# A two-layer approximate-product convolution on one core: images closed two images later, first loads and weight preparation reordered

## The chip, the cores and the metric

The kernel runs on one core of one Trainium2 chip. The core has five engines that work side by side, each through its own list of instructions in order: TensorE (PE in the profile, with PEld for its weight loads), VectorE (DVE), ScalarE (ACT), GpSimd (POOL) and SyncE (SP), which here only issues transfers. They wait for one another by semaphores. The metric is device time in microseconds (us) of one launch; lower is better.

## The reference

The input x has 16 images of 256 channels, 28 x 28, in float32. Each image is group-normalized (32 groups), goes through two convolution layers and comes back with residuals. A layer replaces the 3x3 convolution by centroids: for each channel the nine values of a patch are compared with 16 centroids, a softmax over the negative squared distances gives 16 weights, and the output is the weighted sum of table rows.

```python
d = sum(p*p) - 2*einsum('bncs,cks->bnck', p, centroids) + sum(centroids**2)
attn = softmax(-d, axis=-1)
lut = einsum('cks,cso->cko', centroids, w_sub)
out = einsum('bnck,cko->bno', attn, lut)
```

Layer 1: this, then batch normalization and relu. Layer 2: this on layer 1's result, batch normalization, a squeeze-and-excitation gate (mean over the image, two small matrices, relu, sigmoid), then relu(gated + normalized x) and once more + x. That last line of elementwise work is called the closing of an image below.

## The kernel before

**Tiling.** An image and layer make four blocks: two halves of the channels (hh) times two halves of the rows (t). A block goes through two steps ("clusters" in the code, two per block, eight per image), so image number n of a layer-ordered count (0 to 15 in layer 1, 16 to 31 in layer 2) has its first step at g = 8 n.

**One block.** Patches are loaded from a padded copy in DRAM (`home1`, `home2`) into two buffers `pts` (L317). PE computes logits in eight banks of PSUM (L331), ACT takes exponentials (L348), PE makes the denominator and ninth numerator (`num_b`, L391) and the others (`num_a`, L378). ACT splits the denominator (`split_b`, L405), DVE joins it, takes the reciprocal (L423) and spreads it (L431); ACT copies or DVE scales the numerators (L448, L453), POOL scales the rest (`scale_q`, L444). A block leaves nine operands q of 128 x 392.

**One image.** The four blocks' operands and the 2 x 2 blocks of the weight matrix are multiplied by a Strassen-like scheme of seven products (table `PRODUCTS`, L42). POOL makes the operand differences (`mix`, L470, instructions at L472 and L474), DVE adds and subtracts the results (L499), and ACT normalizes them (L511). Products of image n run in steps g+5 to g+12, so they overlap with the next image's blocks. A product's bank in PSUM is free again when DVE or ACT has read it.

**Order.** Nothing is scheduled by a planner: every piece is entered with `at(step, place, function, ...)` (L813), and the pieces are emitted sorted by step and place (L1001). Each engine executes its instructions in that order, and tile buffers add the waits. A place below 0.5 is logits and the like, 0.5 patch loads, 1.3 to 1.8 the denominators and the spreading, 2.0 the product, 2.5 the mixes. Execution lags the nominal step on some engines.

**Where the change touches.** Loads of the next x (`load_x`, L133) go into the one buffer `xt`. The closing in layer 2 is `finish_norm`, `finish_gate`, `finish_relu` on ACT (L758, L754, L771), `finish_sum` and `finish_add` on POOL (L766, L774) and `store` on SP (L785); the last image instead has `finish_fast` on DVE (L777). Its four output tiles `y` share a ring of four with the padded tiles of layer 1; its normalized x (`xn`) uses tag `pb`, of which there is one buffer, as do the staging tiles `st` and `c2`, layer 2's transposition `z` and the flags' `ok`. In layer 2 the blocks with hh = 0 have a row maximum subtracted for a quarter of their logits (`wide_copy`, `wide_turn`, `wide_sub`, `wide_back`, `wide_exp`).

Layer 2's weights are permuted and prepared during layer 1: `prep_wd*`, `prep_cw*` (L644 to L693) on DVE with loads and stores by SP, and `sums_load`, `sums_put` (L695, L709) with sums on POOL. Layer 1's matrices are combined on DVE at the start (`combine`, L179; `center`, L245; `setup_bn`, L231, which goes back and forth between POOL and DVE).

Of the kernel before, what the change touches and what calls it, by code (L numbers as in the profile page):

```python
# [8 lines left out]
F32 = mybir.dt.float32  # L9
# [8 lines left out]
P = 128  # L18
H = W = 28
HW = H * W  # L20
# [3 lines left out]
N = RT * W  # L24
# [43 lines left out]
def kernel(  # L68
# [20 lines left out]
    nc = tc.nc  # L89
    B, C, _ = x.shape  # L90
    NB = C // P
# [11 lines left out]
    def bank(name):  # L103
        return p_ring.tile([P, 512], F32, tag="ps", name=name)
# [10 lines left out]
    d_cwb = dram.tile([P, 1024], F32, name="d_cwb")  # L115
# [10 lines left out]
    io = ctx.enter_context(tc.tile_pool(name="io", bufs=1))  # L126
    wpool = ctx.enter_context(tc.tile_pool(name="wpool", bufs=1))
    epool = ctx.enter_context(tc.tile_pool(name="epool", bufs=6))
# [1 line left out]

    xs = {}

    def load_x(b, eng=None):  # L133
        t = io.tile([P, NB, HW], F32, tag="xt", name="xt")
        (eng or nc.sync).dma_start(t, x[b].rearrange("(b p) n -> p b n", p=P))
        xs[b] = t

    def load_x0(k):
# [66 lines left out]
    pts = [const.tile([P, 8, PTW], F32, name=f"pt{i}") for i in range(NPT)]  # L205
# [9 lines left out]
    nc.gpsimd.memset(mhalf, -0.5)  # L215
    nc.vector.memset(xpads[0], 0.0)
    nc.gpsimd.memset(xpads[1], 0.0)
    nc.vector.memset(pts[0], 1.0)
    nc.gpsimd.memset(pts[1], 1.0)

    def rsqrt(dst, src, eps, n):
# [42 lines left out]
    def gn_stats(b, k):  # L264
        if k == 0:
            gst[b] = (
                small.tile([P, NB, 2, 6], F32, name="gn_st"),
                small.tile([P, NB, 2], F32, name="gn_mv"),
            )
        st, mv = gst[b]  # L270
        for i in range(2):
            nc.vector.bn_stats(st[:, k, i, :], xs[b][:, k, i * (HW // 2) : (i + 1) * (HW // 2)])
        nc.vector.bn_aggr(mv[:, k, :], st[:, k])

    def gn_mean(b, k0=0, n=NB):
        st, mv = gst[b]
        ps = bank("gnp")[:, : 2 * n]
        nc.tensor.matmul(
            ps, lhsT=gmat, rhs=mv[:, k0 : k0 + n].rearrange("p b t -> p (b t)"), start=True, stop=True
        )  # L280
        gm = small.tile([P, NB, 2], F32, name="gn_gm")
        nc.vector.tensor_copy(gm[:, :n].rearrange("p b t -> p (b t)"), ps)
        dv = small.tile([P, NB], F32, name="gn_dv")
        nc.vector.tensor_sub(dv[:, :n], mv[:, k0 : k0 + n, 0], gm[:, :n, 0])
        nc.vector.tensor_mul(dv[:, :n], dv[:, :n], dv[:, :n])
        gst[b, "m"] = gm, dv
# [16 lines left out]
    def gn_apply(b, k):  # L303
        nc.scalar.activation(
            grid(xpads[k])[:, 1 : H + 1, 1 : W + 1], xs[b][:, k].rearrange("p (r w) -> p r w", w=W), AF.Identity,
            bias=nrm[:, b, 2, k : k + 1], scale=nrm[:, b, 1, k : k + 1],
        )
# [305 lines left out]
    pw = {}  # L613
# [68 lines left out]
            nc.vector.tensor_scalar(f[:, :, 8 * c : 8 * c + 8], src[:, :, 0:8], m_cw[:, c : c + 1], None, op0=ALU.mult)  # L682
        nc.sync.dma_start(d_cwa, st[:, 512:1536])

    def prep_cwb():
        st = pw.pop("st")
        src = st[:, : 32 * S].rearrange("p (m i s) -> p m i s", i=4, s=S)
        f = st[:, 512:1536].rearrange("p (m i n) -> p m i n", i=4, n=32)
        for m in range(8):
            nc.vector.tensor_copy(f[:, m], m_b[:, m % 4, :].unsqueeze(1).to_broadcast([P, 4, 32]))  # L690
            nc.vector.tensor_mul(f[:, m], f[:, m], src[:, m, :, 8:9].to_broadcast([P, 4, 32]))
            nc.vector.tensor_add(f[:, m], f[:, m], ones_b[:, m % 4, :].unsqueeze(1).to_broadcast([P, 4, 32]))
        nc.sync.dma_start(d_cwb, st[:, 512:1536])  # L693

    def sums_load(k0):  # L695
        st = stage()
# [116 lines left out]
    def at(cl, sub, f, *a, **kw):  # L813
        jobs.setdefault((cl, sub), []).append((f, a, kw))
# [7 lines left out]
    for j, u in enumerate(blocks):  # L822
        gi, g = 8 * (j // 4), 2 * j
# [11 lines left out]
    for j, u in enumerate(blocks):  # L835
        g = 2 * j
        u["w"] = j
        wide = u["l"] == 1 and u["hh"] == 0
        for p in range(2):
            u["pt", p] = pts[p]  # L840
            at(g + p - NPT, 0.5, patches, u, p, nc.gpsimd if g + p < 5 else None)
            for q in range(2):
                mm = 2 * p + q
# [25 lines left out]
    for l in range(2):  # L869
        for b in range(B):  # L870
            n = l * B + b
            g = 8 * n
            us = blocks[4 * n : 4 * n + 4]
            for c, (w, r, ks) in PRODUCTS.items():
                at(g + c, 2.0, product, (n, c), us[r], w, ks)
            for mm in (4, 2, 3, 0, 1):
                at(g + 5, 2.5, mix, us[0], mm, us[1], us[0])
                at(g + 7, 2.5, mix, us[1], mm, us[2], us[1])
                at(*((g + 7, 2.6) if l == 0 else (g + 8, 1.0)), mix, us[0], mm, us[2], us[0])
                at(g + 10, 2.5, mix, us[0], mm, us[0], us[3])  # L880
            c11, c12, c21, c22 = (0, 0), (0, 1), (1, 0), (1, 1)
            at(g + 6, 0.0, acc_copy, l, b, c11, (n, 5))
            at(g + 7, 0.0, acc_copy, l, b, None, (n, 6))
            at(g + 8, 0.0, acc_add, l, b, None, (n, 7))
            at(g + 9, 0.0, acc_add, l, b, c21, (n, 8), c11)
            at(g + 10, 0.0, acc_add, l, b, c22, (n, 9), c11, pop=False)
            at(g + 10, 0.01, acc_add, l, b, c21, (n, 9))
            at(g + 10, 0.05, reg_add, l, b, c12, c22, None)
            at(g + 10, 0.06, reg_add, l, b, c22, c21, None)
            at(g + 11, 0.0, acc_add, l, b, c12, (n, 10))  # L890
            at(g + 11, 1.9, norm_out, l, b, *c12)
            at(g + 11, 1.91, norm_out, l, b, *c22)
            at(g + 12, 0.0, acc_add, l, b, c11, (n, 11))
            at(g + 12, 0.3, norm_out, l, b, *c11)
            at(g + 13, 0.0, acc_add, l, b, c21, (n, 12), op=ALU.subtract)
            at(g + 13, 0.3, norm_out, l, b, *c21)
            if l == 0:
                for o in range(2):
                    if b == 0:
                        at(g + 12 + o, 0.35, rank_score, o)  # L900
                        at(g + 12 + o, 0.6, rank_keep, o)
                        at(g + 12 + 2 * o, 0.65, h0_keep, o)
                    else:
                        for r in range(2):
                            at(g + 12 + o + (o and r), (0.5, 2.9)[r] if o == 0 else (2.4, 2.9)[r], to_home2, b, o, r)
                if b + 1 < B:
                    at(*((g - 1, 2.6) if b else (1, 0.7)), load_x, b + 1)
                    for q in range(NB):
                        at(g + (1 if b else 2) + 2 * q, 1.95, gn_stats, b + 1, q)
                    at(g + 4, 1.05 if b else 1.96, gn_mean, b + 1)  # L910
                    at(g + 4, 1.33 if b else 1.97, gn_var, b + 1)
                    for q in range(NB):
                        at(g + 5, 0.9, gn_apply, b + 1, q)
                        at(g + 5, 1.9, to_home1, b + 1, q)
            else:
                at(g + 10, 2.6, load_x, b)
                at(g + 13, 2.1, se_hidden, b)
                at(g + 14, 1.05, se_gate, b)
                for q in range(NB):
                    at(g + 13, 0.9, finish_norm, b, q)  # L920
                    if b < B - 1:
                        at(g + 15, 0.3, finish_gate, b, q)
                        at(g + 15, 0.9, finish_sum, b, q)
                        at(g + 16, 1.9, finish_relu, b, q)
                        at(g + 17, 0.05, finish_add, b, q)
                        at(g + 17, 2.9, store, b, q)
                    else:
                        at(g + 14, 1.92, finish_fast, b, q)
                        at(g + 14, 1.92, store, b, q)
                if b == B - 1:  # L930
                    at(g + 11, 0.95, flags)
                    at(g + 12, 2.9, flag_sum)

    at(2, 0.6, load_w, 0, "A11")
    at(3, 0.6, load_w, 0, "S3")
    at(3, 0.6, load_w, 0, "A22")
    at(5, 0.6, load_w, 0, "A12")
    for n, m in enumerate(("S1", "S2", "S4", "S3")):
        at((4, 5, 7, 6)[n], 1.95, combine, m)
    for hh in range(2):  # L940
        at(6, 2.7, keep_wd, hh)
    for o in range(2):
# [6 lines left out]
    for o in range(2):  # L949
# [5 lines left out]
        for part in range(3):  # L955
            c = 28 + 6 * o + 2 * part
# [4 lines left out]
    at(43, 1.05, prep_wd2)  # L961
    at(46, 0.6, prep_cw0)
    at(47, 1.9, prep_cwa)
    at(48, 1.9, prep_cwb)
    for n in range(5):
        at(50 + 2 * n, 0.6, sums_load, 2 * n)
        at(51 + 2 * n, 2.3, sums_put, 2 * n)
    g = 8 * B
    at(g - 2, 0.4, load_wd, 1, 0)
    at(g, 0.4, load_wd, 1, 1)  # L970
# [9 lines left out]

    for k in range(NB):
        gn_stats(0, k)
        gn_mean(0, k, 1)
        gn_var(0, k, 1)
        gn_apply(0, k)
        if k == 0:
            to_home1(0, 0)
# [4 lines left out]
    center_wd(0)  # L992
    at(-0.5, 0.7, to_home1, 0, 1)
    at(0, 0.6, load_wd, None, 1)
    at(1, 0.6, load_cw, 0, 1)
    at(1, 1.95, center_wd, 1)
    at(3, 1.95, setup_bn)
    for t in hpads:
        at(0, 1.95, nc.gpsimd.memset, t, 0.0)

    for key in sorted(jobs):  # L1001
        for f, a, kw in jobs[key]:
# [5 lines left out]
    with tc.If(rv > 0):  # L1008
        with tc.For_i(0, B, 1) as it:
            t = io.tile([P, NB, HW], F32, tag="xt", name="xt")  # L1010
# [13 lines left out]
            for l in range(2):  # L1024
# [6 lines left out]
                for t2 in range(2):  # L1031
                    us = []
# [125 lines left out]
```

## Time and profile before

| | us |
|---|---|
| time, median of three runs (lowest to highest) | 2848.76 (2846.7 to 2851.04) |
| the profiled execution: its own time | 2846.91 |
| the profiled execution: span from first to last instruction | 2845.4 |
| PE busy in matmuls | 2713.7 |
| POOL busy | 2055.2 |
| DVE busy | 1755.4 |
| ACT busy | 1456.7 |

The profile is one execution, recorded by the hardware. Busy time is that of instructions proper; waiting and the issuing of transfers are not counted. A group line of the profile reads: line of the code, engine, operation, output<-inputs, shape, count | busy us, mean ns of one | idle time of that engine just before, and what ended it. A line of the order of time reads: start, duration, engine, line, operation, tiles, shape, count. A line of the table by stage gives a window of the span, its length, the busy us and instruction count of PE, PE's weight loads, DVE, ACT and POOL, the granted PE clock as a share of full speed, the share of time that the DMA engines were busy, and GB/s. Matmul ends are modelled, so a busy PE is not necessarily at its peak.

### The profile page before, as it was taken

To read this page: it belongs to the slowest core of one execution; us is meant where nothing else is said; L and a number is where in the kernel's file an instruction comes from. 1 tells how busy PE (TensorE), PEld (TensorE's weight loads), DVE (VectorE), ACT (ScalarE), POOL (GpSimd) and SP (SyncE) were. 2 spreads that over 40 slices of the span, in tenths; PEclk is the share of its full clock that TensorE was granted. 3 is DMA by queue.
4 is the path that set the end of the run, shared out by engine and by line. 5 is a ranking of instruction groups with operands and counts; after the bars stand their busy time and mean duration, and the time that the engine had idled before them with its cause. 6 is when DMAs were issued, how large, how long until landed. Compare 5 with 4: busy or idle time off the path is not lost.

```text
span 2845.4 us, 87952 instructions
## 1 busy us (share of the span) xinstructions
PE 2713.7 (95%) x37076; PEld 1284.5 (45%) x37076; DVE 1755.4 (62%) x3973; ACT 1456.7 (51%) x3278; POOL 2055.2 (72%) x1396
## 2 busy tenths in 40 slices
PE   4789999999999999999999999999999999999997
PEld 1344444444444444444444444444444444444443
DVE  4656555675555556555657676666666667766664
ACT  3344455444555544445545556655555555555552
POOL 3647877668776676767667877777977778877776
PEclk8899999999999999999999999999999999999999
DMA  8565677567666655566665544544544555544541
GB/s 193 127 125 120 175 194 189 142 145 182 160 161 159 153 141 126 145 159 149 154 152 112 113 110 100 119 108 109 116 102 104 118 109 114 116 97 109 117 108 36
DMA packets 223009, 374.51 MB, mean 132 GB/s; under 512 B 30136, under 2 KB 193320, under 8 KB 222608
## 3 DMA queue, kind: packets, MB, share of 16 engines
q1 hardware_dynamic: 215376, 334.50, 51.8%
q0 software_dynamic: 7232, 34.30, 3.5%
q8 instruction: 296, 4.85, 0.8%
q14 instruction: 105, 0.86, 0.1%
HBM read 288.91 MB, written 79.80 MB: 130 GB/s over the span
## 4 chain that ended last, share of the span: by engine, by line
PE 61%; POOL 20%; DVE 11%; ACT 4%; issue 2%; DMA 2%; SPq 0%; DVEq 0%; POOLq 0%; ACTq 0%
PE acc L465 32%; PE lg L336 12%; POOL qp L474 11%; PE nb L397 8%; PE na L383 8%; POOL qp L446 3%; ACT e L348 3%; DVE r L423 3%; POOL y L767 2%; DVE rb L438 2%; POOL qo L472 1%; POOL z L368 1%; DVE se_gt L750 1%; DMA pt<-home 1%; DVE qp L457 1%
## 5 line engine op out<-in xcount | busy, mean ns | idle before, releaser
L348 ACT ACTIVATE e<-lg 128x392 f32<-128x392 f32 x1920 | 778.2, 526 | 934.3 <-PE lg L336 934.2
L474 POOL TENSOR_TENSOR qp<-qp,qp 128x784 f32<-128x784 f32 x512 | 936.8, 1864 | 0.0
L465 PE MATMUL acc<-qp,w_S 128*128 128x392 f32 x2048 | 737.6, 502 | 35.4 <-POOL qp L474 35.4
L446 POOL TENSOR_TENSOR qp<-qp,rb 128x784 f32<-128x784 f32 x256 | 472.6, 1869 | 299.3 <-DVE rb L438 299.2
L336 PE MATMUL lg<-pt,wd 32*32 32x392 f32 x16384 | 539.6, 505 | 31.3 <-DVE hpad L502 11.3
L465 PEld LDWEIGHTS acc<-qp,w_S 128*128 128x128 f32 x2048 | 375.8, 190 | 380.7 <-POOL qp L474 123.7
L438 DVE STREAM_SHUFFLE rb<-r 128x392 f32<-128x392 f32 x1024 | 540.5, 605 | 0.0
L465 PE MATMUL acc<-qp,w_A 128*128 128x392 f32 x1536 | 522.3, 493 | 0.2 <-POOL qp L474 0.2
L383 PE MATMUL na<-e,cwa 64*32 64x392 f32 x8192 | 408.6, 498 | 13.2 <-issue 7.4
L465 PEld LDWEIGHTS acc<-qp,w_A 128*128 128x128 f32 x1536 | 292.1, 190 | 215.2 <-POOL qp L474 1.4
L397 PE MATMUL nb<-e,cwb 64*32 64x392 f32 x8192 | 374.1, 500 | 0.0
L336 PEld LDWEIGHTS lg<-pt,wd 32*32 32x32 f32 x16384 | 231.6, 103 | 289.0 <-issue 187.9
L446 POOL TENSOR_TENSOR qo<-qo,rb 128x392 f32<-128x392 f32 x128 | 131.2, 1025 | 316.5 <-DVE rb L434 316.3
L457 DVE TENSOR_TENSOR qp<-na,rb 128x392 f32<-128x392 f32 x512 | 253.1, 558 | 150.5 <-PE na L383 150.3
L423 DVE RECIPROCAL r<-r 128x392 f32<-128x392 f32 x128 | 331.8, 2593 | 0.0
L417 DVE SCALAR_TENSOR_TENSOR r<-nb,kst,r 128x392 f32<-128x392 f32 x128 | 79.8, 623 | 375.9 <-ACT r L408 367.7
L383 PEld LDWEIGHTS na<-e,cwa 64*32 64x32 f32 x8192 | 143.2, 106 | 235.8 <-ACT e L348 119.7
L397 PEld LDWEIGHTS nb<-e,cwb 64*32 64x32 f32 x8192 | 146.6, 108 | 203.1 <-issue 130.9
L451 ACT COPY qp<-na 128x392 f32<-128x392 f32 x512 | 210.8, 505 | 7.1 <-PE na L383 7.1
L408 ACT ACTIVATE r<-nb,kst 128x392 f32<-128x392 f32 x128 | 86.9, 679 | 108.7 <-PE nb L397 103.7
L502 DVE TENSOR_TENSOR y<-acc,y 128x392 f32<-128x392 f32 x80 | 43.5, 561 | 148.7 <-PE acc L465 142.3
L472 POOL TENSOR_TENSOR qo<-qo,qo 128x392 f32<-128x392 f32 x128 | 131.7, 1029 | 0.5
(142 smaller groups left out, 1807.3 us busy)
## 6 DMA issues: line engine op xcount, KB each, us to landing
pt<-home SPq DMA_DIRECT2D x768, 209.0 KB
pt<-home SPq DMA_DIRECT2D x753, 104.5 KB
home<-xpad SPq DMA_DIRECT2D x32, 899.0 KB
xt<-in_x SPq DMA_DIRECT2D x31, 784.0 KB
out_dram<-y SPq DMA_DIRECT2D x32, 392.0 KB
w_S<-d_wS SPq DMA_DIRECT2D x4, 576.0 KB
st<-in_wsub SPq DMA_DIRECT2D x4, 512.0 KB
st<-d_wa SPq DMA_DIRECT2D x16, 128.0 KB
```

The costliest lines, as they stand in the source:

```text
L336: nc.tensor.matmul(bk[32 * c : 32 * c + 32, :N].rearrange("p (r w) -> p r w", w=W), lhsT=wts["wd", u["hh"]][32 * i : 32 * i + 32, mm, c, : ...
L348: nc.scalar.activation(eg[:, i, :], bk[:, :N], AF.Exp, scale=2.0)
L383: nc.tensor.matmul(bs[r][32 * i : 32 * i + 32, :N], lhsT=wts["cwa", u["hh"]][64 * r : 64 * r + 64, mm, i, :], rhs=es[64 * r : 64 * r + 64, ...
L397: nc.tensor.matmul(bs[r][32 * i : 32 * i + 32, :N], lhsT=wts["cwb", u["hh"]][64 * r : 64 * r + 64, mm, i, :], rhs=es[64 * r : 64 * r + 64, ...
L423: nc.vector.reciprocal(u["r"], u["r"])
L438: nc.vector.stream_shuffle(rb[:, r, :], u["r"], mask_of(2 * mm + r))
L446: nc.gpsimd.tensor_tensor(q, q, u.pop(("rb", mm)), ALU.mult)
L451: nc.scalar.copy(u["q", 2 * mm + r], bk[:, :N])
L457: nc.vector.tensor_mul(u["q", 2 * mm + r], bk[:, :N], rb[:, r, :])
L465: nc.tensor.matmul(accs[key][:, :N], lhsT=wl[w][:, k, :], rhs=us["q", k], start=first and n == 0, stop=last and n == len(ks) - 1,)
L472: nc.gpsimd.tensor_tensor(out_u["q", 8], in0["q", 8], in1["q", 8], ALU.subtract)
L474: nc.gpsimd.tensor_tensor(pair(out_u, mm), pair(in0, mm), pair(in1, mm), ALU.subtract)
```

## The change

Five things are done, all by other places in the order and two helper functions:

- Layer 2's closing: x is loaded at g+13 instead of g+10; norm and gate run at step g+19, sum and relu at g+20, add and store at g+21, where they were at g+13 to g+17. The last image keeps its own short closing, and its x goes into a spare tile of the exponentials' pool at g+11.
- The third mix of an image is put behind the next image's first pieces for the last image of layer 1 too, as for layer 2 (the condition was on the layer, and is now n < B - 1).
- At the start: one memset moves behind the first statistics; the second centring, the loads of A11, A12, cwa/cwb and image 1, image 1's group statistics, the four combinations and setup_bn get other steps.
- `prep_cwb`'s 24 operations are split into four parts of six in steps 48 to 51, and the loads and sums after it move two steps on.
- The zeroing of the padded tiles moves from step 0 to step 1.

```diff
-    def load_x(b, eng=None):
-        t = io.tile([P, NB, HW], F32, tag="xt", name="xt")
-        (eng or nc.sync).dma_start(t, x[b].rearrange("(b p) n -> p b n", p=P))
+    def load_x(b, spare=False):
+        if spare:
+            t = epool.tile([P, 4, N], F32, tag="e", name="e").rearrange("p i n -> p (i n)")
+            t = t.rearrange("p (b n) -> p b n", b=NB)
+        else:
+            t = io.tile([P, NB, HW], F32, tag="xt", name="xt")
+        nc.sync.dma_start(t, x[b].rearrange("(b p) n -> p b n", p=P))
...
-    nc.vector.memset(pts[0], 1.0)
...
-    def prep_cwb():
-        st = pw.pop("st")
+    def prep_cwb(part):
+        st = pw["st"]
...
-        for m in range(8):
+        for m in range(2 * part, 2 * part + 2):
...
-        nc.sync.dma_start(d_cwb, st[:, 512:1536])
+        if part == 3:
+            pw.pop("st")
+            nc.sync.dma_start(d_cwb, st[:, 512:1536])
...
-                at(*((g + 7, 2.6) if l == 0 else (g + 8, 1.0)), mix, us[0], mm, us[2], us[0])
+                at(*((g + 7, 2.6) if n < B - 1 else (g + 8, 1.0)), mix, us[0], mm, us[2], us[0])
...
-                    at(*((g - 1, 2.6) if b else (1, 0.7)), load_x, b + 1)
+                    at(g + (-1 if b else 2), 2.6, load_x, b + 1)
                     for q in range(NB):
-                        at(g + (1 if b else 2) + 2 * q, 1.95, gn_stats, b + 1, q)
-                    at(g + 4, 1.05 if b else 1.96, gn_mean, b + 1)
-                    at(g + 4, 1.33 if b else 1.97, gn_var, b + 1)
+                        at(g + (1 + 2 * q if b else 4), 1.95, gn_stats, b + 1, q)
+                    at(g + (4 if b else 5), 1.05, gn_mean, b + 1)
+                    at(g + (4 if b else 5), 1.33, gn_var, b + 1)
                     for q in range(NB):
-                        at(g + 5, 0.9, gn_apply, b + 1, q)
+                        at(g + 5, 0.9 if b else 1.5, gn_apply, b + 1, q)
                         at(g + 5, 1.9, to_home1, b + 1, q)
             else:
-                at(g + 10, 2.6, load_x, b)
+                last = b == B - 1
+                at(*((g + 11, 0.6) if last else (g + 13, 2.6)), load_x, b, last)
...
-                    at(g + 13, 0.9, finish_norm, b, q)
-                    if b < B - 1:
-                        at(g + 15, 0.3, finish_gate, b, q)
-                        at(g + 15, 0.9, finish_sum, b, q)
-                        at(g + 16, 1.9, finish_relu, b, q)
-                        at(g + 17, 0.05, finish_add, b, q)
-                        at(g + 17, 2.9, store, b, q)
+                    at(g + (13 if last else 19), 0.9, finish_norm, b, q)
+                    if not last:
+                        at(g + 19, 0.91, finish_gate, b, q)
+                        at(g + 20, 0.05, finish_sum, b, q)
+                        at(g + 20, 0.9, finish_relu, b, q)
+                        at(g + 21, 0.05, finish_add, b, q)
+                        at(g + 21, 0.06, store, b, q)
...
-    at(2, 0.6, load_w, 0, "A11")
+    at(1, 0.6, load_w, 0, "A11")
...
-    at(5, 0.6, load_w, 0, "A12")
-    for n, m in enumerate(("S1", "S2", "S4", "S3")):
-        at((4, 5, 7, 6)[n], 1.95, combine, m)
+    at(6, 0.6, load_w, 0, "A12")
+    for c, m in ((5, "S1"), (7, "S2"), (8, "S4"), (6, "S3")):
+        at(c, 1.96, combine, m)
...
-    at(48, 1.9, prep_cwb)
+    for part in range(4):
+        at(48 + part, 1.9, prep_cwb, part)
     for n in range(5):
-        at(50 + 2 * n, 0.6, sums_load, 2 * n)
-        at(51 + 2 * n, 2.3, sums_put, 2 * n)
+        at(52 + 2 * n, 0.6, sums_load, 2 * n)
+        at(53 + 2 * n, 2.3, sums_put, 2 * n)
...
     for k in range(NB):
         gn_stats(0, k)
+        if k == 0:
+            nc.vector.memset(pts[0], 1.0)
...
-    at(1, 0.6, load_cw, 0, 1)
-    at(1, 1.95, center_wd, 1)
-    at(3, 1.95, setup_bn)
+    at(2, 2.6, load_cw, 0, 1)
+    at(2, 1.95, center_wd, 1)
+    at(7, 1.97, setup_bn)
     for t in hpads:
-        at(0, 1.95, nc.gpsimd.memset, t, 0.0)
+        at(1, 1.95, nc.gpsimd.memset, t, 0.0)
```

## The prediction

> **What bounds the kernel now.** I read the page first, then a table by stage cut at each image's first logits matmul, then the instructions of one layer-2 image in order of time. Lines of the page:
>
> ```profile
> span 2845.4 us, 87952 instructions
> ...
> PE 2713.7 (95%) x37076; PEld 1284.5 (45%) x37076; DVE 1755.4 (62%) x3973; ACT 1456.7 (51%) x3278; POOL 2055.2 (72%) x1396
> ...
> L465 PE MATMUL acc<-qp,w_S 128*128 128x392 f32 x2048 | 737.6, 502 | 35.4 <-POOL qp L474 35.4
> ```
>
> TensorE (PE) bounds it: it idles 131.7 us in all, and 35.4 us of that is the product waiting for the operand differences that GpSimd (POOL) makes at L474. The stages (window, then busy us of PE, weight load, VectorE (DVE), ScalarE (ACT), POOL, granted clock, DMA):
>
> ```profile
> 25.40:105.80 80.40, 58.46 (x942) 24.46 (x943) 42.70 (x107) 37.17 (x86) 30.80 (x33) 0.83 0.81 188
> 105.80:213.20 107.40, 90.50 (x1156) 41.61 (x1157) 63.71 (x148) 42.46 (x96) 57.49 (x39) 0.90 0.55 114
> 744.30:827.20 82.90, 82.67 (x1155) 39.96 (x1154) 48.18 (x123) 42.16 (x96) 59.02 (x43) 1.00 0.61 150
> 563.90:659.50 95.60, 88.57 (x1158) 40.81 (x1159) 65.56 (x152) 42.36 (x96) 66.56 (x52) 0.95 0.69 167
> 1409.10:1499.30 90.20, 86.52 (x1152) 39.70 (x1152) 55.42 (x118) 43.19 (x96) 63.26 (x41) 0.96 0.70 161
> 1499.30:1583.50 84.20, 83.35 (x1163) 39.68 (x1162) 57.00 (x120) 47.36 (x107) 61.11 (x38) 1.00 0.49 105
> 1583.50:1669.60 86.10, 84.12 (x1168) 39.45 (x1168) 57.19 (x120) 48.88 (x109) 66.58 (x41) 1.00 0.50 110
> ```
>
> They are: images 0 and 1; image 8 (a steady one of layer 1, 82.9); image 6, with the weight preparation (95.6); layer 2's first image (90.2), its second (84.2), its third (86.1). From the third to the last but one each takes 86.1. The second differs in one thing: no earlier image is closed beside it. So closing costs 1.9 us an image, and this view measures what is to be had. Its place, POOL at the end of an image:
>
> ```profile
> 2011.28 3.69 POOL L767 TENSOR_TENSOR y<-y,xn 128x784 f32<-128x784 f32 x2 [1.92 <-ACT y L756]
> 2014.91 3.72 POOL L446 TENSOR_TENSOR qp<-qp,rb 128x784 f32<-128x784 f32 x2
> 2018.58 1.04 POOL L472 TENSOR_TENSOR qo<-qo,qo 128x392 f32<-128x392 f32 x1
> 2019.56 7.29 POOL L474 TENSOR_TENSOR qp<-qp,qp 128x784 f32<-128x784 f32 x4
> ```
>
> The closing sum (L767) stands ahead of the scaling (L446) and of the differences that the next product reads. That product's four groups wait 0.62, 0.23, 0.22 and 0.23 us in the third image.
>
> Weight preparation, on DVE and on POOL:
>
> ```profile
> 576.22 7.35 POOL L474 TENSOR_TENSOR qp<-qp,qp 128x784 f32<-128x784 f32 x4
> 578.51 1.49 DVE L690 COPY st<-kst 128x128 f32<-128x128 f32 x1
> 580.03 1.85 DVE L691 TENSOR_TENSOR st<-st 128x128 f32<-128x128 f32 x1
> 581.91 1.81 DVE L692 TENSOR_TENSOR st<-st,kst 128x128 f32<-128x128 f32 x1
> 583.54 1.06 POOL L446 TENSOR_TENSOR qo<-qo,rb 128x392 f32<-128x392 f32 x1
> 583.65 1.03 DVE L690 COPY st<-kst 128x128 f32<-128x128 f32 x1
> 584.72 0.29 DVE L691 TENSOR_TENSOR st<-st 128x128 f32<-128x128 f32 x1
> 585.04 0.29 DVE L692 TENSOR_TENSOR st<-st,kst 128x128 f32<-128x128 f32 x1
> ```
>
> An operation of 0.22 to 0.29 us takes 1.5 to 1.85 while POOL works: each ends with a POOL operation.
>
> **What the Trainium skill says.** "SBUF — State Buffer", section "Who interferes with whom": DVE copies and tensor_scalar in a two-port mode, and tensor_tensor with both inputs in SBUF, share a port pair with GpSimd as an exclusive lock; the second comer waits out the whole instruction. The trace agrees (1.85 against 0.29). "TensorE: Matmul & The Clock Gate", Part 1: an idle array is throttled to half clock and needs busy time to recover. The trace agrees: after the 8.4 us wait at 31.8 the clock is 0.5 until 47.8. "DMA: Bandwidth & Descriptors", "Anatomy of one DMA": a wait holds the issuing sequencer, not the DMA engine, so SP's order counts; SP stands at one patch load from 87.5 to 96.4.
>
> **Closing of layer 2 (14 images, slots 18 to 31).** Removed from steps 7 to 9 (counted from an image's g): gate, sum, relu, add, stores; added at steps 3 to 5 of the image after next. POOL loses two sums (3.7) ahead of the scaling. The scaling then waits for its reciprocal rows instead, so only 1.8 of the 3.7 come through; the second image shows just this, the last difference 1.8 us earlier against its PE. Gain 86.1 - 84.2 = 1.9.
> New costs: ACT in step 3 gets norm (2.0) and gate (1.85). It was idle 3.6 us before step 4's first exponential, so that is late by 0.25; PE's next bank waits about 0.2. In step 4 the relus (1.65) stand before split_b, which moves from 1549.87 to about 1551.6; POOL is free for the sums at 1546.6, so they end at 1548.5 and 1550.3, in time. join_b, reciprocal (2.6) and spreads follow 1.75 late, and the DVE add that frees a product's bank ends at 1559.3 instead of 1557.8, where PE's numerators want to start at 1559.1: 0.3 at most. POOL's adds fit a gap of 7.2 us. SP: two stores and load_x now stand ahead of patches. The patches of step 5 issue some 2.8 late but land 5 us before use; a store lands 2.2 to 2.4 us after issue in the trace, 5 us ahead of the acc_copy that takes its buffer. All hidden; without that cover a late patch costs PE its lateness one to one. Net 1.9 - 0.5 = 1.4 an image, x14 = **-20** (0.8 to 1.9: -11 to -26).
>
> **First layer-2 image.** Its predecessor's third mix goes behind wide_sub on POOL. Before, wide_sub ran only at 1428.5, wide_back held DVE, and PE spent 8.2 us on logits of 2.0 and 4.9 on num_b of 2.9 (half clock): 8.2 too much. The product after now waits for the mix as in slot 17, about 1. **-7** (-3 to -8).
>
> **Weight preparation in four parts.** Before: 24 operations, 11.6 us, in one piece, 18 of them fast because POOL had run dry. Parts of six meet a working POOL each time. Part 0, as shown: 6.9. Part 1, beside two scalings: 0.9 + 1.8 + 4 x 0.28 = 4.0. Part 2, beside a mix of 7.3: four operations to its end, then 0.6: 7.9. Part 3 like part 1: 4.0. Sum 22.8, twice the old. DVE reaches the bank-freeing adds of step 50 at 596.0 (596.6 before), so that stall stays (-0.5, and -1 in clock), and those of step 52 at 626.5 with PE wanting them at 619.8: +6.7 and 1.5 of half clock. The sums' loads, two steps later, add one more POOL block before a mix: +0.3, and a late patch load seen once at 659.5, +1.0. Sum about **+7**. If POOL gave way instead, the stall would go: -11; if starvation as in L549 (5.5 us for 0.25) recurs, +10.
>
> **Start.** The memset (2.86) moves behind the first statistics; x lands at 4.29 and these ran at 5.52, but the copy after the first group matmul now waits for the memset (8.4 for 7.5), of which POOL's own memset hides most: +0.35. Hidden memsets of the border on POOL: 0. PE waited 31.8 to 40.2 for the second weight centring; now it runs image 0's second logits when their patches land (37.6). But centring is queued on DVE behind join, reciprocal and spreads, so PE waits again, about 46 to 52.7: +0.8 by num_b of block 1. The statistics of image 1 move off PE's way: wait 8.4 becomes about 1.5 to 3, product 5 starts at 78.0 for 82.9: -4.9. Loads in order of use (A11 first, image 1 and cwa/cwb later) land 5 us or more before use: 0. setup_bn at step 7 is new trouble: its DVE half waits for POOL operations queued after two scalings, so the add that frees half_sum's bank goes from 110.9 to 115.3: +4.4; combine S4 in step 8 costs 1.3, less 2.2 because code_spread's L549 waits less: -0.9. Sum 0.35 - 4.9 - 0.35 + 4.4 - 0.9 = **-1.4** (-10 to +6, half-clock windows being coarse).
>
> **End.** POOL loses 1.8 and the add of 3.7; PE then binds, and the last product ends 2.1 earlier. But image 14's closing buffer is the one that the flags take (one buffer of that tag), and flags are written before its sum is queued: DVE waits for POOL's sum (about 2827.0), the flags follow, then the last accumulator add, then ACT's relus (1.65) ahead of the last norm: the hidden layer of the gate comes 1.0 later than 2833.4. **+1** (-2 to +4).
>
> Sum -20 - 7 + 7 - 1.4 + 1 = -20.4. The profiled execution took 2846.91 (span 2845.4 and 1.5 around it): 2826.5. The median, 2848.76, lies 1.9 higher: **2828**.
>
> **Rivals.** (1) The parts of the preparation find POOL idle or ahead, so its stall goes (-11 for +7), and the start gains more: 2828 - 18 = 2810. For it: 18 of 24 operations were fast. Against: POOL was idle then only because DVE held it. (2) No difference: ACT's lumps in steps 3 and 4 cost 1.9 us an image, all that they free; the rest of the sum is -0.4: 2848. For it: PE's slack at step 5 is 0.2 us. (3) Slower: POOL's sums hold ACT. The relus wait for them, and split_b, the copies and PE's banks are behind. The margin is 0.5 us (1550.3 against ACT at 1550.85); if sums come 2 us later than I place them, PE loses 1.5 an image and the sum is zero (20.4 / 14); at 3.5 it loses 3: 14 x 3 = 42 more than 2828, 2870. Against: POOL had gaps of 7 to 8 us in these steps. (4) That images are closed later but the mixes not earlier can't be: the second image shows it.
>
> **How the numbers follow.** Main 0.60, own range 2818 to 2840; rival 1 0.20, 2806 to 2818; no difference 0.08, 2843 to 2854; slower 0.12 including smaller losses of the third mechanism, to 2875. Main and rival 1 hold 0.8: 2806 to 2841. A measurement tells 0.2% (5.7 us) from no change: faster 0.82, same 0.08, slower 0.10.
>
> **What would show it.** Layer-2 images 84.4 to 85.2 long, with no waits of the first product after a boundary; L336 without its 3.5 us at 1433; L690 to L692 with means well over the present 0.48 us and a PE stall some 50 us into image 6; a DVE wait in setup_bn near 110 us; flags after L767. Images at 86 or more, with ACT waiting for POOL at the relus, would make it wrong; so would an image 6 under 88.

## The result and the profile after

The kernel after took 2830.25 us (median of four runs, 2828.01 to 2834.27) against 2847.73 for the kernel before (2846.28 to 2851.04). The ratio is 0.9939, with a 95% interval of 0.9921 to 0.9956, so 17.5 us less. The forecast was 2828. The profiled execution of after took 2834.27 (span 2832.8), the longest of its four; against the profiled 2846.91 of before that is 12.6 less, and the comparisons by stage below add up to this smaller difference.

Lines of the page after:

```profile
span 2832.8 us, 88059 instructions
...
PE 2710.9 (96%) x37076; PEld 1288.5 (45%) x37076; DVE 1742.4 (62%) x3974; ACT 1454.5 (51%) x3277; POOL 2057.2 (73%) x1396
...
L468 PE MATMUL acc<-qp,w_S 128*128 128x392 f32 x2048 | 729.0, 500 | 20.2 <-POOL qp L477 19.9
```

PE waits 19.9 us for POOL's operand differences, where it waited 35.4. The table by stage, in the order of that of before (images 0, 1, 8, 6, then layer 2's first, second and third; columns as there):

```profile
26.70:102.60 75.90, 57.47 (x944) 24.92 (x945) 39.08 (x97) 37.11 (x86) 29.01 (x29) 0.89 0.88 202
102.60:212.20 109.60, 89.17 (x1155) 40.78 (x1155) 66.36 (x157) 42.37 (x96) 63.07 (x46) 0.92 0.52 102
756.50:839.40 82.90, 82.67 (x1157) 39.94 (x1156) 48.06 (x123) 42.14 (x96) 59.02 (x43) 1.00 0.60 151
564.80:671.20 106.40, 92.41 (x1161) 41.62 (x1162) 76.55 (x151) 42.28 (x96) 62.75 (x47) 0.90 0.56 142
1423.20:1506.80 83.60, 82.74 (x1156) 39.01 (x1157) 55.48 (x118) 43.08 (x96) 63.35 (x41) 1.00 0.75 174
1506.80:1591.00 84.20, 83.35 (x1165) 39.67 (x1164) 56.99 (x120) 43.85 (x103) 59.12 (x37) 1.00 0.48 105
1591.00:1675.90 84.90, 84.04 (x1169) 39.74 (x1170) 55.74 (x120) 48.75 (x109) 66.98 (x41) 1.00 0.51 112
```

Three rows carry the result. Layer 2's third image takes 84.9 instead of 86.1, and images 18 to 30 take 84.66 on average instead of 86.09: 13 x 1.43 = 18.6 us gained. Layer 2's first image takes 83.6 instead of 90.2. Image 6, with the weight preparation, takes 106.4 instead of 95.6: 10.8 us lost, while image 8 and the second layer-2 image are unchanged. Image 0 is shorter (75.9 for 80.4), image 1 longer (109.6 for 107.4); the first logits stand at 26.7 instead of 25.4, and image 4 starts at 389.4 instead of 389.1, so the start comes out even. The end is 1.5 shorter (from image 31's first logits to PE's last matmul 130.5 for 132.0, to the end of the program 141.2 for 142.7). Images 4, 5 and 7 together take 1.2 more. Image 13 takes 87.9 instead of 85.6, with 3.4 us of half clock that the kernel before doesn't show there. The change doesn't touch that image: in the runs below it takes 85.7 to 88.5, with the old order as with the new, so it can't be laid to the change.

The preparation's three groups on DVE (last columns: busy us, mean ns of one, idle us before):

```profile
L694 DVE TENSOR_TENSOR st<-st 128x128 f32<-128x128 f32 x8 | 10.0, 1255 | 0.3
L693 DVE COPY st<-kst 128x128 f32<-128x128 f32 x8 | 7.4, 929 | 0.0
L695 DVE TENSOR_TENSOR st<-st,kst 128x128 f32<-128x128 f32 x8 | 5.4, 671 | 0.3
```

10.0 + 7.4 + 5.4 = 22.8 us, as forecast; it was 11.6. What PE waited for in image 6 (us in total, times, longest), after:

```profile
PE lg L339 <- DVE hpad L505: 7.3, 3, 6.3
PE na L386 <- DVE hpad L505: 6.3, 1, 6.3
PE acc L468 <- POOL qp L477: 0.3, 1, 0.3
```

And before:

```profile
PE lg L336 <- DVE hpad L502: 5.6, 2, 2.8
PE lg L336 <- DMA st<-d_wa: 1.0, 1, 1.0
PE acc L465 <- POOL qp L474: 0.4, 2, 0.3
```

L505 is the DVE addition that empties a product's bank (L502 before); it stands behind the preparation on DVE. The waits are 13.9 us instead of 7.0, +6.9. The rest of image 6's loss is clock: at a granted 0.90 instead of 0.95, the same work keeps PE busy 92.41 us instead of 88.57, +3.8.

### The profile page after: what moved, and what is told of

Same layout as the page of the kernel before. It is cut to its first block, busy times and chain, and to the rows that moved or that the text cites. A ratio compares the mean times of both kernels' runs of the same rounds, so it can differ in the third digit from the quotient of the medians.

```text
span 2832.8 us, 88059 instructions
## 1 busy us (share of the span) xinstructions
PE 2710.9 (96%) x37076; PEld 1288.5 (45%) x37076; DVE 1742.4 (62%) x3974; ACT 1454.5 (51%) x3277; POOL 2057.2 (73%) x1396
## 5 line engine op out<-in xcount | busy, mean ns | idle before, releaser
L468 PE MATMUL acc<-qp,w_S 128*128 128x392 f32 x2048 | 729.0, 500 | 20.2 <-POOL qp L477 19.9
L357 ACT COPY e<-lg 128x392 f32<-128x392 f32 x128 | 52.9, 500 | 173.6 <-PE lg L339 173.6
```

Source lines behind the costliest of these rows:

```text
L468: nc.tensor.matmul(accs[key][:, :N], lhsT=wl[w][:, k, :], rhs=us["q", k], start=first and n == 0, stop=last and n == len(ks) - 1,)
```

## The experiments

They ran on other chips of the same kind, where the kernel before took 2861 to 2864 us and a steady layer-1 image 83.5 instead of 82.9; layer-2 images took the same. So each run is compared with the kernel before on its own chip, by the ratio (95% interval in brackets), and image by image. One of the runs is the kernel after itself:

> The kernel after once more, beside the others on this chip: ratio 0.9939 to the kernel before as measured, image 6 at 106, images 18 to 30 at 84.6 to 84.9.

Ratio 0.9937 [0.9925, 0.9950], 2844.24 for 2863.97. Image 6 took 104.7, images 18 to 30 84.78 on average. The result holds, on chips that are slower by half a per cent.

**The preparation in four parts, alone, in the kernel before.**

```diff
-    at(48, 1.9, prep_cwb)
+    for part in range(4):
+        at(48 + part, 1.9, prep_cwb, part)
     for n in range(5):
-        at(50 + 2 * n, 0.6, sums_load, 2 * n)
-        at(51 + 2 * n, 2.3, sums_put, 2 * n)
+        at(52 + 2 * n, 0.6, sums_load, 2 * n)
+        at(53 + 2 * n, 2.3, sums_put, 2 * n)
```

> The kernel before with only the weight preparation cut into four parts (and the sums' loads two steps later with it). Theory A (each of the 24 vector operations is held by whatever POOL runs at that moment; in one piece POOL runs dry beside them, in four parts it does not): the operations take about 22.8 us instead of 11.6, image 6 grows from 95.6 to 106-107, and the kernel is 10 to 12 us slower. Theory B (image 6 grew for another reason, such as the first loads or setup_bn moved, and the parts as such hide): no slower than 3 us, or faster by up to 11.

Ratio 1.0032 [1.0020, 1.0043], +5.7 to +12.3 us. Image 6 took 106.4 (95.3 and 94.5 in the two runs below that keep the old preparation on such chips), and the 24 operations took 22.8 us (10.0, 7.4 and 5.4 as above). The next run undoes the same cut in the kernel after.

> The kernel after with the preparation in one piece again at step 48 and the sums at steps 50 to 59. Theory A: image 6 back to 95-96, the whole 10 to 12 us below the kernel after, so some 28 below the kernel before (ratio 0.990). Theory B: as the kernel after, within 3 us, or above it by up to 11.

Ratio 0.9909 [0.9894, 0.9925], 26.4 below the kernel before by medians; image 6 took 94.8. So the parts cost image 6 its 10 to 12 us, and this change would have been worth some 8 us more without them (0.9937 - 0.9909 = 0.0028 of 2861; 10 to 12 was expected). In both runs the sums' loads move with the parts, but they are not the cause: in the kernel after the first moved sum runs on POOL at 654.9, after both of image 6's long stalls, which end at 586.8 and 618.4.

**Why the parts cost: their sum, or six in a row?** First the same 24 operations, one in a step (operation i % 3 of m = i // 3), in the kernel after.

```diff
-    for part in range(4):
-        at(48 + part, 1.9, prep_cwb, part)
+    for i in range(24):
+        at(48 + i // 1, 1.9, prep_cwb, i)
...
+        at(72 + 2 * n, 0.6, sums_load, 2 * n)
+        at(73 + 2 * n, 2.3, sums_put, 2 * n)
```

> The kernel after with the same 24 vector operations of the preparation, one in each step from 48 to 71 (the sums' loads from step 72). Theory A (PE stalls because six held operations in a row overrun the slack that a step leaves the vector engine): the operations still take some 15 to 30 us in all, yet no step is overrun; image 6 takes 83 to 87 instead of 106, image 7 and 8 within 1 us of theirs; 19 to 22 us below the kernel after. Rival (it is their total of held time that counts, wherever they stand): within 4 us of the kernel after.

Ratio 0.9885 [0.9871, 0.9900]. The operations still took 7.2 + 6.8 + 5.8 = 19.8 us, 0.83 each, and image 6 87.8, image 7 84.6. So nearly the same held time, spread, costs image 6 little: 87.8 is 3.8 above the 84.0 of the last version below, where the four parts are about 21 above it. The expectation missed at two places. Image 6 is 0.8 over its range, with one wait of 1.7 us at the addition behind the first copy, a step after `prep_cwa`'s lump of 6.3 us, and 3.4 us of half clock. And from the ratio the gain is about 15 us instead of 19 to 22: image 10, where sums now fall, took 86.0 instead of 83.5, with 1.9 us of waits for POOL's differences (0.2 in the kernel after), and image 8, which now holds a part of the preparation, took 1.2 more.

Then six operations, each for four values of m at once (128 x 512), one in a step:

```diff
-            nc.vector.tensor_mul(f[:, m], f[:, m], src[:, m, :, 8:9].to_broadcast([P, 4, 32]))
+            nc.vector.tensor_mul(f[:, h], f[:, h], src[:, h, :, 8:9].to_broadcast([P, 4, 4, 32]))
...
+    for i in range(6):
+        at(48 + i // 1, 1.9, prep_cwb, i)
```

> The kernel after with the preparation in 6 operations of four times the size, one in each step from 48 to 53 (the sums from step 54). Theory A (the hold is per operation, up to one POOL operation of 1.85 us each): 6 to 12 us for the operations, no step overrun by more than 0.5; image 6 takes 83 to 87; 19 to 22 us below the kernel after. Rival (a larger operation is held over several POOL operations, or holds POOL): image 6 at 90 to 100, 6 to 15 us below.

Ratio 0.9877 [0.9862, 0.9891]. Its three groups:

```profile
L694 DVE COPY st<-kst 128x512 f32<-128x512 f32 x2 | 2.8, 1416 | 0.0
L698 DVE TENSOR_TENSOR st<-st,kst 128x512 f32<-128x512 f32 x2 | 2.4, 1192 | 0.0
L696 DVE TENSOR_TENSOR st<-st 128x512 f32<-128x512 f32 x2 | 1.5, 766 | 0.0
```

6.7 us instead of 22.8 for the same elements: 1416, 1192 and 766 ns for four times the work that took 929, 671 and 1255 ns. Both runs put one operation in a step, and one of four times the size takes 1.12 us on average where a small one takes 0.83. So the hold goes by the operation, not by the element. It is the port rule of the Trainium skill, "SBUF — State Buffer", section "Who interferes with whom" (the blocked one waits for the other's whole instruction), counted per instruction. Image 6 took 84.8, 19.9 less than in the kernel after; the whole gained about 17 by the ratio, where 19 to 22 was expected. Images 7 and 8 together took 2.3 more (171.8 for 169.5): in image 8 PE waits 0.9 us for POOL's differences, as it doesn't in the kernel after, and the last sums on POOL now run there (742.6). That they are the reason was not tested alone.

**The closing alone, in the kernel before.** `load_x`, norm, gate, sum, relu, add and store of layer 2 as in the change, all else as before.

```diff
-                at(g + 10, 2.6, load_x, b)
+                at(*((g + 11, 0.6) if last else (g + 13, 2.6)), load_x, b, last)
...
-                        at(g + 15, 0.3, finish_gate, b, q)
-                        at(g + 15, 0.9, finish_sum, b, q)
+                        at(g + 19, 0.91, finish_gate, b, q)
+                        at(g + 20, 0.05, finish_sum, b, q)
```

> The kernel before with only the closing of a layer-2 image (load, norm, gate, sum, relu, add, store) moved to its successor's last steps. Theory A (POOL's two sums ahead of the scaling delay the next product by 1.9 us an image, ACT's lumps give 0.5 back): images 18 to 30 take 84.6 to 84.8 instead of 86.1, in all -20 us (-18 to -21; the tail between -1 and +1). Theory B (the gain of the layer-2 images came with the earlier mix): 0 to -3.

Ratio 0.9945 [0.9932, 0.9959], -19.5 to -11.7 us where -18 to -21 was expected. By images the gain is as expected: 18 to 30 took 84.71 on average, and the end was 1.5 shorter as in the kernel after, so 13 x 1.38 + 1.5 = 19.4; the first layer-2 image, where the old mix stayed, took 91.1, 0.9 more than before.

**The earlier mix alone, in the kernel before.**

```diff
-                at(*((g + 7, 2.6) if l == 0 else (g + 8, 1.0)), mix, us[0], mm, us[2], us[0])
+                at(*((g + 7, 2.6) if n < B - 1 else (g + 8, 1.0)), mix, us[0], mm, us[2], us[0])
```

> The kernel before with only the third mix of layer 1's last image put behind the wide block's subtraction on POOL. Theory A: only the first layer-2 image moves, from 90.2 to 83.5-84, so -6 to -7 us, and images 18 to 30 stay at 86.1. Theory B (the mix belongs to the closing's gain): images 18 to 30 shorter too, more than -10 in all.

Ratio 0.9974 [0.9967, 0.9982], -9.4 to -5.1 us. The first layer-2 image took 84.1, images 18 to 30 stayed at 86.09. The two parts of layer 2 are independent and add up.

**Is it POOL's work that made the old closing dear?** The kernel after, with two more sums on POOL (`again`: y = y + y, 128 x 784, the gate halved to make up for it) at the old place:

```diff
                         at(g + 19, 0.91, finish_gate, b, q)
+                        at(g + 15, 0.9, again, b, q, "pool")
```

> The kernel after with two more POOL sums of the same size (y + y, with the gate halved to make up for it) where the closing sums stood before, at step 7 of the image's successor; norm, gate, relu, add and stores stay late. Theory A (the closing cost its 1.4 us an image by POOL's two sums ahead of the scaling): images 18 to 30 back from 84.65 to 85.9-86.1, in all 16 to 20 us above the kernel after. Rival (ACT's gate and norm at their old places were the cost): within 4 us of the kernel after.

Ratio 0.9944 [0.9932, 0.9957]: nothing lost. Images 18 to 30 took 84.72. My theory, as I had put it, fell. POOL around the boundary after image 22 in this run, then in the kernel after:

```profile
2021.74 2.94 POOL L769 TENSOR_TENSOR y<-y 128x784 f32<-128x784 f32 x2
2025.73 3.69 POOL L449 TENSOR_TENSOR qp<-qp,rb 128x784 f32<-128x784 f32 x2 [1.04 <-DVE rb L441]
```

```profile
2013.69 3.69 POOL L449 TENSOR_TENSOR qp<-qp,rb 128x784 f32<-128x784 f32 x2 [3.94 <-DVE rb L441]
```

POOL has 3.94 us to spare there, since the rows that the scaling needs (rb) are not ready. The added sums wait for nothing, fill 2.94 of it, and the scaling starts when its rows are there, as without them. In the kernel before the closing sums (L767 in the prediction's lines) first waited 1.92 us for ACT's gate at the same place. They started at 2011.28 and ended at 2014.91, while the second row that the scaling needs was written by 2013.2. Without that wait they would have started at 2009.36 and ended at 2013.05, in time. So the traces point to the sums' wait for the gate at the head of POOL's queue, not to their 3.7 us of work alone, as what the change took off the path. This is argued from three traces and not shown by a run: none had the gate earlier at the old place. The added sums, with one operand twice, took 2.94 and not 3.69, which is also below the 3.94.

**And ACT's work?** The kernel after, with two pairs of copies of y onto itself on ACT (`again`, 128 x 784), in steps 5 and 7 of the image's successor:

```diff
                         at(g + 19, 0.91, finish_gate, b, q)
+                        at(g + 13, 2.2, again, b, q, "act")
+                        at(g + 15, 0.3, again, b, q, "act")
```

> The kernel after with two pairs of ACT copies of y onto itself where norm and gate stood before (steps 5 and 7 of the image's successor), 1.9 us each pair; POOL unchanged. Theory A: images 18 to 30 stay within 0.3 of 84.65, the whole within 4 us of the kernel after. Rival (ACT's place was the cost): 16 to 20 us above it.

Ratio 1.0008 [1.0000, 1.0015], 20.3 us above the kernel after by medians. Images 18 to 30 took 86.15 on average (most 85.76, three 87.4 with a stretch of half clock). That is not the old cost come back, though. The pair at step 7 left POOL's scaling with its 3.95 us of idle time. The pair at step 5 I had put at another place than the old norm: behind the gate's hidden layer, which waits for PE, and ahead of the copy that frees a product's bank. ACT in this run, then in the kernel after on the same chip:

```profile
1844.00 0.25 ACT L740 ACTIVATE se_hid<-sep,b_sb 16x1 f32<-16x1 f32 x1 [5.57 <-PE sep L734]
1844.15 1.59 ACT L768 ACTIVATE y<-y 128x784 f32<-128x784 f32 x2
1845.65 0.46 ACT L499 COPY y<-acc 128x392 f32<-128x392 f32 x1
```

```profile
1840.00 0.25 ACT L740 ACTIVATE se_hid<-sep,b_sb 16x1 f32<-16x1 f32 x1 [5.58 <-PE sep L734]
1840.16 0.46 ACT L499 COPY y<-acc 128x392 f32<-128x392 f32 x1
```

The copy L499 comes 1.5 us later after the hidden layer, and PE's next logits wait for it. The list of waits gives 0.34 an image, but the image is 1.0 to 1.1 longer, and all of that arises there: set logits against logits, image 21 is 0.2 us behind the kernel after's just ahead of that place and 1.2 just behind it. The old norm stood just ahead of that hidden layer, inside ACT's idle time there, with 3.3 us of it still left behind the norm. So this run doesn't test the rival it was made for, and whether ACT's norm and gate at their old places had a share in the old cost stays open. It shows that 1.6 us on ACT just behind an instruction that waits for PE can cost 1.1 us, although ACT sits idle 5.6 us just ahead of it.

**setup_bn.** The kernel after with it back at step 3:

> The kernel after with only setup_bn back at step 3. Theory A (its vector half holds the add that frees half_sum's bank behind POOL's queue at step 7): the wait of 12.2 us near 117 falls to about 4, code_spread's 5 us return as in the kernel before, and step 3 pays up to 2: net -2 to -5 us. Rival (the start's stalls come from the order of the loads): within 2 us.

Ratio 0.9943 [0.9930, 0.9956]. The wait fell from 12.2 to 3.9 as expected, images 0 and 1 took 181.6 together instead of 185.5 in the kernel after on these chips, but image 4 starts at 391.4 for 391.9. The time can't be told from the kernel after's, where 2 to 5 us less was expected. Then all of it on POOL, at step 7:

```diff
...
-            nc.vector.tensor_mul(sc, sc, ga)
-            nc.vector.tensor_mul(sh, mu, sc)
-            nc.vector.tensor_sub(sh, be, sh)
+            nc.gpsimd.tensor_tensor(sc, sc, ga, ALU.mult)
+            nc.gpsimd.tensor_tensor(sh, mu, sc, ALU.mult)
+            nc.gpsimd.tensor_tensor(sh, be, sh, ALU.subtract)
```

> The kernel after with all of setup_bn's small operations on POOL at step 7, none on the vector engine. Theory A: the vector engine's queue no longer waits for POOL there; the wait of 12.2 us near 117 falls to 4 to 6; -4 to -9 us, less what returns in code_spread (up to 5). Rival (POOL's own lateness is the cause): the wait stays at 10 or more, and the time within 2 us.

Ratio 0.9941 [0.9929, 0.9954], again no different from the kernel after's. PE's waits around steps 7 and 8 in the kernel before, in the kernel after (as first profiled), and then here:

```profile
PE na L383 <- DVE hpad L502: 5.8, 1, 5.8
PE lg L336 <- DVE half_sum L502: 3.8, 1, 3.8
```

```profile
PE lg L339 <- DVE half_sum L505: 12.2, 1, 12.2
PE na L386 <- DVE hpad L505: 0.8, 1, 0.8
```

```profile
PE na L386 <- DVE hpad L505: 6.2, 1, 6.2
PE lg L339 <- DVE half_sum L505: 3.9, 1, 3.9
```

8.3 us of the wait behind half_sum go and 5.4 come back one step later, at `code_spread`, whose DVE operations then meet a working POOL: the same exchange that the change made the other way round (3.8 to 12.2, and 5.8 to 0.8).

**A version that uses this.** Preparation (also `prep_cwa`) in single large operations at the beginning of a step, where DVE waits for PE or ACT anyway; the sums clear of the ends of images; setup_bn on POOL and `code_spread` in the same early place; and at the end the flags and the last image's normalized x in tiles of their own, so that neither waits for image 14's, the last image's x loaded a step earlier, and image 14's relus ahead of the last norm.

```diff
-    at(47, 1.9, prep_cwa)
-    for part in range(4):
-        at(48 + part, 1.9, prep_cwb, part)
-    for n in range(5):
-        at(52 + 2 * n, 0.6, sums_load, 2 * n)
-        at(53 + 2 * n, 2.3, sums_put, 2 * n)
+    for c in range(4):
+        at(48 + c, 0.2, prep_cwa, c)
+    for i in range(6):
+        at(54 + i, 0.2, prep_cwb, i)
+    for n, c in enumerate((64, 66, 68, 72, 74)):
+        at(c, 0.6, sums_load, 2 * n)
+        at(c + 1, 2.3, sums_put, 2 * n)
...
-        at(6 + 2 * o, 1.9, code_spread, o)
+        at(7 + 2 * o, 0.2, code_spread, o)
...
-        ok = io.tile([P, 1568], F32, tag="pb", name="ok")[:, : 16 * B].rearrange("p (a n) -> p a n", a=2)
+        ok = epool.tile([P, 4, N], F32, tag="e", name="e").rearrange("p i n -> p (i n)")[:, : 16 * B].rearrange("p (a n) -> p a n", a=2)
...
-                    at(g + (13 if last else 19), 0.9, finish_norm, b, q)
+                    at(*((g + 11, 1.95) if last else (g + 19, 0.9)), finish_norm, b, q)
...
-                        at(g + 20, 0.9, finish_relu, b, q)
+                        at(g + 20, 0.1 if b == B - 2 else 0.9, finish_relu, b, q)
```

> The kernel after with: the preparation in single large operations at the beginning of a step (where the vector engine idles), the sums clear of the steps before an image's end; setup_bn on POOL and code_spread in the same early gap; the flags and the last image's norm in buffers of their own, the second last image's relus ahead of the last norms. Expected: image 6 at 84-85 (-21), images 5, 7 and 8 together -3 to -5, start -3 to -8, the end -2 to -3: 27 to 37 us below the kernel after, ratio to the kernel before 0.981 to 0.985. Rival (each hold only moves to the next waiting operation): not below six operations one a step, ratio 0.9877.

2816.20 us for 2863.97, ratio 0.9842 [0.9829, 0.9854], and 28.0 below the kernel after beside it. Its image 6:

```profile
564.00:648.00 84.00, 83.77 (x1158) 40.26 (x1157) 53.37 (x127) 42.37 (x96) 58.80 (x43) 1.00 0.63 161
```

Image 6 takes 84.0 with PE at full clock. Against the kernel after on that chip, image 4 starts 5.8 earlier, images 5 to 7 take 22.9 less (20.7 of it image 6), and from image 31's first logits to the end of the program it takes 138.4 instead of 141.5. Images 5, 7 and 8 together gain 2.1, where 3 to 5 was expected. The two profiled executions lie 33.0 apart, the medians 28.0. PE's waits at the two places of the exchange above are 3.9 and 3.3. The parts of this version were not run one by one.

## Why the prediction was right

The sum was -20.4 from the profiled 2846.91, so 2826.5, and 2828 by the median; 2830.25 was measured. That the two medians lie so near is in part luck: between the profiled executions, from which the terms were worked out, the difference is 12.6 and not 20.4. The closing, the first layer-2 image and the DVE time of the preparation came out as worked out. The preparation's stall was priced too low, the start's gain did not show, and image 13's 2.3 us came on top. Two sums of the working don't close: the preparation's terms as listed make +8.0 and were put as about +7, and in the start the +0.8 of the centring stands nowhere in the sum, while a -0.35 stands only there.

- **Closing, -20.** Measured -18.6 over images 18 to 30, -20.0 from the middle of the first layer-2 image to the last logits. The 0.5 us an image taken off is there too, as 84.66 is 0.4 above the second image's 84.2; that ACT's lumps are the reason isn't shown (PE's listed waits are 0.9 us in the third image and 0.8 in the second). The path was right: the sums delayed the scaling by 1.7 us (2014.91 for 2013.2), the differences followed, and PE's waits for them fell from 17.3 us between 1850 and 2600 to 7.1. The size was right because it was taken from the second image. But the step "POOL loses two sums (3.7) ahead of the scaling" put the delay down to the sums' work. Work of that kind fits POOL's idle time there, as the added sums show; by the traces it was the wait of 1.92 us for ACT's gate that made them late. The line quoted in the prediction showed that wait; I read past it to the duration.
- **First layer-2 image, -7.** Measured -6.6, and -5.1 to -9.4 alone.
- **Preparation, +7.** The part that failed, by size. The DVE time was 22.8 as computed part by part, and PE's waits grew by 6.9, against +6.7 and -0.5. But the clock was put at 1.5 less 1, and measured +3.8 in PE's busy time. The two stalls of 2.8 us before stood close together and shared one stretch of half clock of 10.2 us; the two of 6.3 after stand apart, with stretches of 10.2 and 6.8, and one of 3.4 more follows: 20.5 us in all. The Trainium skill, "TensorE: Matmul & The Clock Gate", Part 1, says that activity releases the throttle; the trace agrees (the first stall ends at 586.8, and the clock is half until 592.2), and the term should have been counted stall by stall. Neither stall stands where the working had it: they end at 586.8, where numerators wait for the bank, and at 618.4, instead of 596.0 and 626.5. The patch load, +1.0, did not come. In all +10.8.
- **Start, -1.4.** Measured +0.3 on the first chip. On the others the six runs with the kernel after's first 46 steps start image 4 at 387.8 to 393.0 (mean 390.5), the three with the kernel before's at 392.4 to 393.4 (mean 392.9). The scatter is as large as the term. In it, setup_bn's +4.4 was +8.4 (12.2 for 3.8) and code_spread's return 5.0 instead of 2.2: both ends of the exchange were too small, by 4.0 and 2.8. The first logits were 1.3 late, not 0.35.
- **End, +1.** Flags came after POOL's sum of image 14 as said (2814.04 after 2814.01), but the end as a whole was no later: from the last logits on it took 62.7 for 62.8.

The first rival (the parts find POOL idle) is out by the measured 22.8 us. The second (ACT's lumps eat all that is freed) is out by images of 84.66. The third (ACT held by the relus) did not occur: ACT's relus waited for nothing in any image.

## What to carry to other kernels

In this kernel, small VectorE operations beside a busy GpSimd were priced by their number and not by their elements, and each held lump had to fit the slack of the one step that it stood in. Image 6 took 84.0 or 84.8 with six large operations, 87.8 with 24 in steps of their own, 94.8 with them in one piece beside which POOL ran dry, and 104.7 in lumps of six. So count instructions, and compare each lump with its step. An operation in an in-order queue takes up its wait for an operand as well as its work: before such work is moved, see whether it would fit the engine's idle time if it didn't wait. A stall of PE is priced with the clock behind it.

## What the runs showed that I had not expected

A stall of PE cost about half as much again: +6.9 us of waits came with +3.8 us of longer matmuls in image 6. And 1.6 us on ACT cost 1.1 us an image from just behind an instruction that waits for PE, where ACT sits idle 5.6 us just ahead of it.
